# A fixed order for the first transfers, later loads and degree sums held in order, and one-off weight sums moved into the loop, in a two-layer graph kernel

## The chip, the cores and the metric

One Trainium2 chip, one core. The metric is device time of one execution in microseconds (us). Each kernel is run several times and the median is quoted. A kernel is timed in rounds together with the kernel before on the same chip. Ratios and their intervals are taken from the fast runs of both kernels in the same rounds, so they are not quite the ratio of the medians quoted beside them.

In the profile's lines PE is TensorE, DVE VectorE, ACT ScalarE, POOL GpSimd and SP SyncE; a q behind the name marks the issue of a transfer. A line of a timeline gives start and length (us), engine, source line, operation, what is written <- what is read, and the count; brackets give the idle time before it and what ended it. Line numbers are those of the kernel that is profiled. A line of waits gives who waited <- for what: total us, times, longest us.

## The reference, cut to what matters

64 graphs of 256 nodes and 512 features, float32. Two layers, each with a residual and a norm:

```python
# layer 0
deg = jnp.sum(adj, axis=-1, keepdims=True)
agg = jnp.einsum('bij,bjf->bif', adj, x) / jnp.maximum(deg, EPS)
x = _layernorm(x + relu(concat([x, agg]) @ W.T))
# layer 1
q, k = split(x @ Wqk);  v = x @ Wv
agg = jnp.einsum('bij,bjd->bid', adj, k * mask)
w = inv_scale * mask * sum(q * agg)
x = _layernorm(x + softmax(w)[:, :, None] * v)
```

## The kernel before

Matrix products are done with seven block products in place of eight, so each operand needs a few sums and differences of its blocks first. Those of the weights W (and of W1 = [Wqk Wqk^T, Wv]) are made once, on VectorE. Those of x^T and adj are made for each graph on GpSimd. `prepare(g)` also makes the row sums of adj ("degree sums") on ScalarE, which evicts most of TensorE's results as well (it copies them out of the banks in which TensorE accumulates).

The kernel is written in program order, but a scheduler may move an instruction ahead of earlier ones on its engine if it estimates it to be ready sooner. The resulting order on each engine is fixed when the program is built and can be listed before a run ("the built order" below). `tc.keep_in_program_order(i)` keeps i behind what is traced before it on its engine. `tc.issue_after(i)` keeps a block's instructions on i's engine behind i. Both fix an order of issue only, and add no wait.

```python
def load(g):                                            # all in SP's queue
    xTs[g] = ...; nc.sync.dma_start(xTs[g], x_t[g]...)   # 512 KB
    adjs[g] = ...; nc.sync.dma_start(adjs[g], ...)       # 256 KB, bufs=4
    rows[g] = ...; nc.sync.dma_start(rows[g], ...)       # 256 KB, bufs=2
    xs[g] = ...; nc.sync.dma_start(xs[g], ...)           # 512 KB, bufs=3
# ...
for a in range(NA):
    nc.scalar.dma_start(wqk...[a], src)                 # 4 x 512 KB, ACT's queue
load(0)
for h in (0, 1):
    nc.scalar.dma_start(w0[half h], ...)                # 2 x 1 MB, ACT's queue
# ... the mask, 64 KB
nc.sync.dma_start(w1[:, NF:, :], wv...)                 # 1 MB
# 16 matmuls Wqk Wqk^T into 4 banks (each float32 matmul shows as two in the
# profile: 32), evicted into w1 by ScalarE
# ...
def weight_sums(w, name):                               # VectorE, 128x1024 each
    nc.vector.tensor_sub(t1, b12, b11)
    nc.vector.tensor_sub(t2, b22, t1)
    nc.vector.tensor_sub(b12, b22, b12)
    nc.vector.tensor_sub(t4, b21, t2)

def layer0_a(g):
    product(u, A11, B11);  nc.scalar.copy(own[:, 0, :], u)      # first eviction
    product(p5, S1, T1)
    product(u, S2, T2, start=False);  nc.scalar.copy(y[:, 0, :], u)
    product(p2, A12, B21);  nc.vector.tensor_add(own[:, 0, :], p2, own[:, 0, :])
    product(u, S3, T3, start=False);  nc.scalar.copy(y[:, 1, :], u)   # third eviction
    nc.vector.tensor_add(y[:, 1, :], p5, y[:, 1, :])            # first y addition
def layer0_b(g):
    product(u, A22, T4, start=False);  nc.scalar.copy(own[:, 1, :], u)
    product(p5, S4, B22, start=False)
    nc.vector.tensor_add(y[:, 0, :], p5, y[:, 0, :])            # second y addition
# gather_a(g): four tv sums of the values on VectorE, aggregation adj @ values
# norm0(g):    norm, then two masked copies of x1 on ScalarE (layer 1's values)
W0 = weight_sums(w0, "t0_");  prepare(0);  load(1);  W1 = weight_sums(w1, "t1_")
for i in range(B + G + 2):
    load(i + 2)
    layer0_a(i); ...; layer0_b(i); ...; gather_a(i) mixed with layer 1 of graph i - 2
    combine0(i); norm0(i); prepare(i + 1)
```

## Time and profile before

| | before |
|---|---|
| median, us (three runs) | 2011.91 (2011.75 to 2013.03) |
| TensorE busy | 1973.9 of 2010.2 us |
| TensorE idle in the first 80 us | 15 us |
| TensorE idle in the last 50 us | 21 us |
| TensorE idle between | none |

I follow four landmarks in each profile, all start times of TensorE work: the first Wqk matmul, the first matmul of W (graph 0), the first aggregation matmul of graph 0, and that of graph 1. Before, they stand at 6.18, 22.48, 42.74 and 61.20 us. After some 80 us TensorE never waits until the end, so what is won at the landmarks should arrive at the end. The profile's lines are shown and read in the prediction.

### The profile page before, as it was taken

What the parts mean: (1) busy time and instruction counts of PE and PEld (TensorE: products, weight loads), DVE (VectorE), ACT (ScalarE), POOL (GpSimd) and SP (SyncE); (2) the same over time, 40 slices, a digit from 0 to 9 for tenths busy, and PEclk for the clock granted to TensorE, in tenths of its full rate; (3) what the DMA queues carried; (4) which work ended last, traced back from release to release, by engine and by line L of the source; (5) the groups of instructions that cost most, each with busy time, mean ns of one, the idle gap of its engine ahead of it and who ended that gap; (6) DMA issues with size and microseconds to landing.
All of it is one profiled execution on the core that took longest, in us unless ns stands there. A gap on an engine that the chain in (4) does not pass through costs nothing.

```text
span 2010.2 us, 19340 instructions
## 1 busy us (share of the span) xinstructions
PE 1973.9 (98%) x5536; PEld 1030.4 (51%) x5536; DVE 1523.6 (76%) x3184; ACT 673.2 (33%) x1354; POOL 419.0 (21%) x518
## 2 busy tenths in 40 slices
PE   7999999999999999999999999999999999999995
PEld 3555555555555555555555555555555555555552
DVE  3677787777787777787777887777877777877776
ACT  2333333333333332333332333333333333333322
POOL 4121221221221222212212212212212212222100
PEclk9999999999999999999999999999999999999998
DMA  7333333333333333323333333333333333233211
GB/s 241 85 71 94 88 79 94 86 82 91 88 81 92 90 80 84 99 77 86 90 87 86 80 94 89 79 94 85 81 92 90 81 91 86 68 79 79 62 38 53
DMA packets 384872, 174.40 MB, mean 87 GB/s; under 512 B 283776, under 2 KB 349440, under 8 KB 384768
## 3 DMA queue, kind: packets, MB, share of 16 engines
q1 hardware_dynamic: 382624, 168.97, 32.0%
q10 hardware_dynamic: 2144, 4.19, 0.6%
q8 instruction: 46, 0.75, 0.2%
q14 instruction: 58, 0.48, 0.1%
HBM read 105.97 MB, written 33.55 MB: 69 GB/s over the span
## 4 chain that ended last, share of the span: by engine, by line
PE 95%; DVE 1%; ACT 1%; SPq 0%; issue 0%; DMA 0%; DVEq 0%; ACTq 0%
PE mm L142 75%; PE mm L240 19%; SPq L157 0%; PE tp L349 0%; PE tp L335 0%; DVE st L164 0%; DVE o L357 0%; DVE own L272 0%; ACT L341 0%; ACT vals L281 0%; DMA x1T<-sq 0%; ACT rows L177 0%; DVE o L170 0%; DVE own L274 0%; DVE v L325 0%
## 5 line engine op out<-in xcount | busy, mean ns | idle before, releaser
L142 PE MATMUL mm<-w,s 128*128 128x512 f32 x1024 | 481.3, 592 | 0.7 <-ACT v L311 0.7
L142 PE MATMUL mm<-t,s 128*128 128x512 f32 x1024 | 466.2, 597 | 4.8 <-ACT own L197 3.8
L142 PEld LDWEIGHTS mm<-t,s 128*128 128x128 f32 x1024 | 192.3, 190 | 236.7 <-issue 215.5
L142 PEld LDWEIGHTS mm<-w,s 128*128 128x128 f32 x1024 | 194.4, 190 | 192.8 <-issue 163.2
L142 PE MATMUL mm<-w,x1T 128*128 128x512 f32 x512 | 242.5, 596 | 4.1 <-DMA x1T<-sq 4.1
L142 PE MATMUL mm<-w,xT 128*128 128x512 f32 x512 | 242.0, 594 | 0.0
L183 POOL TENSOR_TENSOR sa<-adj 128x128 f32<-128x128 f32 x64 | 47.1, 736 | 781.0 <-PE mm L240 774.3
L134 POOL TENSOR_TENSOR s<-xT 128x256 f32<-128x256 f32 x64 | 47.7, 745 | 703.6 <-PE mm L142 685.8
L240 PE MATMUL mm<-tv,sa 128*128 128x256 f32 x768 | 187.1, 379 | 0.0
L240 PEld LDWEIGHTS mm<-tv,sa 128*128 128x128 f32 x768 | 145.8, 190 | 74.6 <-issue 59.6
L142 PEld LDWEIGHTS mm<-w,xT 128*128 128x128 f32 x512 | 97.9, 191 | 95.8 <-issue 92.4
L272 DVE SCALAR_TENSOR_TENSOR own<-zr,rdeg,own 128x512 f32<-128x512 f32 x128 | 107.6, 841 | 44.4 <-ACT zr L262 44.4
L319 DVE TENSOR_TENSOR v<-mm,v 128x512 f32<-128x512 f32 x64 | 44.3, 692 | 126.3 <-ACT v L318 126.3
L142 PEld LDWEIGHTS mm<-w,x1T 128*128 128x128 f32 x512 | 95.3, 191 | 86.1 <-issue 74.6
L300 DVE SCALAR_TENSOR_TENSOR q<-mm,zr 128x512 f32<-128x512 f32 x128 | 87.7, 685 | 66.1 <-PE mm L142 66.1
L311 ACT COPY v<-mm 128x512 f32<-128x512 f32 x64 | 37.4, 585 | 299.0 <-PE mm L142 299.0
L142 PE MATMUL mm<-t,x1T 128*128 128x512 f32 x256 | 125.5, 612 | 0.7 <-ACT v L318 0.7
L142 PE MATMUL mm<-t,xT 128*128 128x512 f32 x256 | 120.6, 593 | 3.0 <-ACT vals L204 3.0
L240 PE MATMUL mm<-vals,adj 128*128 128x256 f32 x512 | 121.3, 379 | 1.6 <-DVE vals L214 1.6
L357 DVE SCALAR_TENSOR_TENSOR o<-v,probs,x 128x512 f32<-128x512 f32 x128 | 120.3, 959 | 0.1
L240 PEld LDWEIGHTS mm<-vals,adj 128*128 128x128 f32 x512 | 97.1, 190 | 43.2 <-issue 21.5
L214 DVE TENSOR_TENSOR vals<-mm,vals 128x512 f32<-128x512 f32 x64 | 44.3, 692 | 91.8 <-PE mm L142 91.8
(83 smaller groups left out, 2668.6 us busy)
## 6 DMA issues: line engine op xcount, KB each, us to landing
xT<-x_t SPq DMA_DIRECT2D x64, 512.0 KB, 4.1
x<-x SPq DMA_DIRECT2D x64, 512.0 KB, 3.5
x1T<-sq SPq DMA_DIRECT2D x1024, 32.0 KB, 2.0
out<-o SPq DMA_DIRECT2D x64, 512.0 KB, 3.1
adj<-adj_t SPq DMA_DIRECT2D x64, 256.0 KB, 2.6
rows<-adj SPq DMA_DIRECT2D x64, 256.0 KB, 2.6
wqk<-wqk_t ACTq DMA_DIRECT2D x4, 512.0 KB, 8.6
w<-w_t ACTq DMA_DIRECT2D x2, 1024.0 KB, 11.7
```

Source lines behind the costliest of these rows:

```text
L134: eng.tensor_add(s1, a21, a22)
L142: nc.tensor.matmul(ps, a[:, c, :], b[:, c, :], start=start and c == 0, stop=(c == H - 1), skip_group_check=True)
L183: nc.gpsimd.tensor_add(sa[:, 0], a21, a22)
L214: nc.vector.tensor_add(y[:, 0, :], p5, y[:, 0, :])
L240: nc.tensor.matmul(ps[:, k * HF:(k + 1) * HF], sumsA[g - k][a], w[b][:, n, :], start=start and n == 0, stop=True, skip_group_check=True)
L272: nc.vector.scalar_tensor_tensor(own[:, t, :], z[:, t, :], rdeg[:, t:t + 1], own[:, t, :], op0=OP.mult, op1=OP.add)
L300: nc.vector.scalar_tensor_tensor(q, a, 1.0, agg[:, t, :], op0=OP.mult, op1=OP.mult, accum_out=to)
L311: nc.scalar.copy(v[:, 0, :], u)
L319: nc.vector.tensor_add(v[:, 1, :], p5, v[:, 1, :])
L357: nc.vector.scalar_tensor_tensor(o[:, t, :], v[:, t, :], p[:, t, g % G:g % G + 1], x1[:, t, :], op0=OP.mult, op1=OP.add)
```

## The change

Its intent is to have TensorE start earlier and not be held by its first operands. All first transfers go through one queue in the order in which they are used (Wqk, two quarters of W, x^T of graph 0, the other quarters of W, and then the rest). Loads of graph i+2 are issued behind the last of graph i+1, and degree sums of graph i+1 behind graph i's first eviction. The W1 sums move from before the loop to step 1.

```diff
+    def first(out, in_):
+        return tc.keep_in_program_order(nc.sync.dma_start(out, in_))
-    def load(g):
-        xTs[g] = ...  # first of the four
+    def load(g, dma=nc.sync.dma_start):     # adj, rows, x, then x^T through load_t(g, dma)
...
-            nc.scalar.dma_start(wqk...[a], src)
-        load(0)
-        for h in (0, 1):
-            nc.scalar.dma_start(w0[:, h * NF:(h + 1) * NF, :], ...)
+            first(wqk...[a], src)
+        for k in (0, 2):
+            first(w0[:, k * H:(k + 1) * H, :], w0_of[k])
+        load_t(0, first)
+        for k in (3, 1):
+            first(w0[:, k * H:(k + 1) * H, :], w0_of[k])
+        load(0, first)
         mask_sb = ...
-        nc.sync.dma_start(w1[:, NF:, :], wv...)
+        load_t(1, first)
+        load(1, first)
+        loaded = first(w1[:, NF:, :], wv...)
...
-    load(1)
-    W1 = weight_sums(w1, "t1_")
...
         if i + 2 < B:
-            load(i + 2)
+            with tc.issue_after(loaded.ins):
+                loaded = load(i + 2)
+        if i == 1:
+            W1 = weight_sums(w1, "t1_")
...
-            layer0_a(i)
+            began = layer0_a(i)              # returns the first eviction
...
         if i + 1 < B:
-            prepare(i + 1)
+            with tc.issue_after(began.ins):
+                prepare(i + 1)
```

More of the change, by code (lines that the diff above doesn't have):

```diff
@@ L76, in resnorm_kernel, with load_t @@
      open0) = ({} for _ in range(17))
-    def load(g):
-        xTs[g] = pool.tile([P, NF, N], F32, name="xT")
-        nc.sync.dma_start(xTs[g], x_t[g].rearrange("(c p) n -> p c n", p=P))
+    def first(out, in_):
+        return tc.keep_in_program_order(nc.sync.dma_start(out, in_))
+    def load(g, dma=nc.sync.dma_start):
         adjs[g] = pool.tile([P, NT, N], F32, name="adj", bufs=4)
-        nc.sync.dma_start(adjs[g], adj_t[g].rearrange("(t p) i -> p t i", p=P))
+        dma(adjs[g], adj_t[g].rearrange("(t p) i -> p t i", p=P))
         rows[g] = pool.tile([P, NT, N], F32, name="rows")
-        nc.sync.dma_start(rows[g], adj[g].rearrange("(t p) j -> p t j", p=P))
+        dma(rows[g], adj[g].rearrange("(t p) j -> p t j", p=P))
         xs[g] = pool.tile([P, NT, F], F32, name="x", bufs=3)
-        nc.sync.dma_start(xs[g], x[g].rearrange("(t p) f -> p t f", p=P))
+        dma(xs[g], x[g].rearrange("(t p) f -> p t f", p=P))
+        return load_t(g, dma)
+    def load_t(g, dma):
+        if g not in xTs:
+            xTs[g] = pool.tile([P, NF, N], F32, name="xT")
+            return dma(xTs[g], x_t[g].rearrange("(c p) n -> p c n", p=P))
     w0 = const.tile([P, 2 * NF, F], F32, name="w0")
@@ L95, in resnorm_kernel @@
             src = wqk_t.rearrange("(h a p) f -> a p h f", p=P, h=2)[a]
-            nc.scalar.dma_start(wqk.rearrange("p (h a) f -> a p h f", h=2)[a], src)
-        load(0)
-        for h in (0, 1):
-            nc.scalar.dma_start(w0[:, h * NF:(h + 1) * NF, :],
-                                w_t[h * F:(h + 1) * F, :].rearrange("(c p) o -> p c o", p=P))
+            first(wqk.rearrange("p (h a) f -> a p h f", h=2)[a], src)
+        w0_of = w_t.rearrange("(k h p) o -> k p h o", p=P, h=H)
+        for k in (0, 2):
[4 more added lines that the diff above has]
+        load(0, first)
         mask_sb = const.tile([P, NT, B], F32, name="mask_sb")
-        nc.sync.dma_start(mask_sb, mask_t)
-        nc.sync.dma_start(w1[:, NF:, :], wv.rearrange("(c p) o -> p c o", p=P))
+        first(mask_sb, mask_t)
+        load_t(1, first)
+        load(1, first)
+        loaded = first(w1[:, NF:, :], wv.rearrange("(c p) o -> p c o", p=P))
         ident = const.tile([P, P], F32, name="ident")
@@ L196, in layer0_a @@
         product(u, s["A11"], w["B11"])
-        nc.scalar.copy(own[:, 0, :], u)
+        began = nc.scalar.copy(own[:, 0, :], u)
         product(p5, s["S1"], w["T1"])
@@ L206, in layer0_a @@
         open0[g] = u, p5
+        return began
     def layer0_b(g):
```

## The prediction

> **What bounds the kernel now.** I read the page's busy table first, then a table of stretches, then TensorE's waits over the whole run, and last the first 60 us in order of time.
>
> ```profile
> span 2010.2 us, 19340 instructions
> PE 1973.9 (98%) x5536; PEld 1030.4 (51%) x5536; DVE 1523.6 (76%) x3184; ACT 673.2 (33%) x1354; POOL 419.0 (21%) x518
> ```
>
> TensorE is busy for 1973.9 of 2010.2 us. All its idle time together is 36.3 us, or 1.8% of the span: no better order of loads can win more than that without also raising the clock. The table of stretches (columns: stretch, length, busy us and count of each engine, granted TensorE clock, DMA share, GB/s) shows where it lies:
>
> ```profile
> 0.00:10.00 10.00, 3.82 (x5) 1.76 (x6) 0.06 (x1) 0.00 (x0) 2.70 (x11) 1.00 0.79 273
> 20.00:30.00 10.00, 6.31 (x15) 2.29 (x13) 6.60 (x7) 3.92 (x13) 6.43 (x4) 1.00 1.03 349
> 30.00:40.00 10.00, 8.83 (x16) 3.65 (x17) 7.74 (x12) 5.89 (x23) 7.47 (x9) 0.83 0.45 131
> 200.00:1000.00 800.00, 800.00 (x2258) 418.96 (x2257) 619.46 (x1298) 273.45 (x552) 174.40 (x212) 1.00 0.33 86
> 1980.00:2010.20 30.20, 14.24 (x31) 5.85 (x29) 12.35 (x33) 5.47 (x9) 0.00 (x0) 0.73 0.11 42
> ```
>
> The middle is saturated: 800.00 busy in 800.00, at full clock. The idle sits in the first 80 us (about 15 us) and in the last 50 (about 21). The change rewrites the start, so the start is what can be won. TensorE's waits within the first 80 us:
>
> ```profile
> PE mm L113 <- DMA wqk<-wqk_t: 6.2, 1, 6.2
> PE mm L142 <- ACT own L197: 3.8, 1, 3.8
> PE mm L142 <- ACT vals L204: 3.0, 3, 2.1
> PE mm L240 <- DVE vals L214: 1.6, 2, 0.8
> PE mm L142 <- DVE t L122: 0.4, 1, 0.4
> ```
>
> They sum to 15.0 us. In order of time they are the first matmul waiting for Wqk until 6.18; the wait for T1 of W; and the 3.8 us for the eviction of graph 0's first product. ScalarE's timeline tells why that eviction was late:
>
> ```profile
> 26.00 1.06 ACT L116 COPY w<-mm 128x512 f32<-128x512 f32 x2
> 29.02 0.42 ACT L177 ACTIVATE rows<-rows 128x256 f32<-128x256 f32 x1 [1.96 <-DMA rows<-adj]
> 29.34 0.19 ACT L177 ACTIVATION_READ_ACCUMULATOR rows<-rows 128x1 f32 x1
> 29.43 0.40 ACT L177 ACTIVATE rows<-rows 128x256 f32<-128x256 f32 x1
> 29.74 0.19 ACT L177 ACTIVATION_READ_ACCUMULATOR rows<-rows 128x1 f32 x1
> 29.83 0.56 ACT L197 COPY own<-mm 128x512 f32<-128x512 f32 x1
> ```
>
> The product was complete at about 24.4. ScalarE had degree sums of later graphs placed ahead of its eviction, sat idle 1.96 us for their rows to land, and evicted at 29.83. TensorE could not accumulate the next product into that bank before. Eleven loads of rows are issued within the first 60 us, where graphs 0 to 2 would do.
>
> **What the Trainium skill says.** Four places bear on it.
> - "DMA: Bandwidth & Descriptors", section "Queues, rings and completion order": each DMA engine round-robins, packet by packet, between the queue rows that have work, and SP and ACT own one row each. The trace agrees: by 6.0 us the ACT queue had moved 0.54 MB and the SP queue 0.67 MB, so the first 512 KB of Wqk shared the engines with x^T, adj, rows and x, which nothing needs yet.
> - "TensorE: Matmul & The Clock Gate", section "What's actually happening": the array starts at half clock, about 3.4 us of sustained work releases it, an idle window throttles it again, and the window is free-running. The trace agrees: the first six matmuls start 0.85 us apart, later ones 0.43, and after the 3.8 us wait they are 0.85 apart again for some five matmuls, where the clock column shows 0.83 (for the first ten microseconds it shows 1.00, so there I go by the spacing).
> - The same page, "Architectural detail": ScalarE and VectorE are strict FIFO. The eviction behind the late rows, above, is that rule at work.
> - "SBUF — State Buffer", section "SBUF: two separate sides": a VectorE operation with two SBUF inputs and a GpSimd one that reads SBUF exclude each other. Here the same subtraction on W took 1.23 us alone and up to 1.74 beside GpSimd, and GpSimd's 0.72 us sums became 1.7.
>
> **The change part by part.**
>
> (a) Wqk first, in SP's queue alone. In a view of the first 12 us in slices of 0.3 us, the DMA engines moved 0.17 MB up to 3.3 us and then about 385 GB/s. If all of it is Wqk's first quarter (0.52 MB), that is complete at 3.3 + 0.35/0.385 = 4.2, and with its signal the first matmul starts at about 4.4 in place of 6.18. The other quarters follow at 1.4 us each, while a quarter's 8 matmuls take at least 8 x 0.43 = 3.4: no further wait. The 32 matmuls took 22.48 - 6.18 = 16.3 us; with the same warm-up they end at 20.7. Gain 1.8.
>
> (b) W and x^T of graph 0 next. Before, at most eight transfers were outstanding (the mask's issue waited for the first Wqk), so W was issued only at 8.87 and 10.05 and its second half landed at 23.4. Now W's four quarters and x^T are the 2.5 MB behind Wqk's 2.1 MB: the last W quarter lands at about 3.3 + 4.55/0.385 = 15, adj and rows at 16.5, x at 18. VectorE's four subtractions (4 x 1.23, at most 1.74 each) end by 18.5; GpSimd's eight sums (4 x 0.72 + 4 x 0.45 = 4.7, somewhat more with the port shared) by about 19. All lie before 20.7. The wait for T1 goes: from 24.2, when the matmul could have started, to 24.77, it is 0.57.
>
> (c) Degree sums behind the graph's own first eviction. Rows of graphs 1 and up can no longer stand ahead of the eviction of graph 0. It then lies under the S1 x T1 product (4 x 0.43 = 1.72, against 0.56 for a copy), as designed. Without it the next product would have started at 24.77 + 1.72 = 26.49 and not at 30.50: 4.0. And without that idle the clock stays up: the eight matmuls from 30.50 took until 35.70, 5.20 in place of 8 x 0.43 = 3.44: 1.8.
>
> Check of (b) and (c): from 22.48 to graph 0's first aggregation matmul at 42.74 were 20.3 us for 28 matmuls. The floor is 28 x 0.43 = 12.0, plus two exposed evictions that stay (2.56 - 1.72 = 0.84 at vals L204, 2.66 - 1.72 = 0.94 at vals L214), or 13.8. Difference 6.4 = 0.6 + 4.0 + 1.8. So aggregation starts at 20.7 + 13.8 = 34.5, 8.2 us earlier.
>
> (d) Graph 1. Its wait of 2.10 us for vals L204 comes from ScalarE's order: rows (0.6 us), a table load of 1.28, the root, two mask copies, then the eviction. With the rows gone from there the table load can lie under the norm statistics; that may save up to 1.0. I take 0.5. The 0.8 for vals L214 stays.
>
> (e) The T sums of Wqk Wqk^T and Wv move from before the loop to step 1. They are four VectorE operations, about 6 us with the port shared; Wv is last of 8.5 MB and lands at about 25. VectorE is nearly idle between 25 and 34, so most of it fits; one of 1.2 to 1.7 us may stand just ahead of an addition that the aggregation waits for. I take 0.3 of loss.
>
> (f) The middle. Loads keep count and size, and each is needed a step (30 us) after its issue; TensorE has no idle there. Zero. The last 21 us have no loads or degree sums. Zero.
>
> Sum: 1.8 + 6.4 + 0.5 - 0.3 = 8.4, so 2011.9 - 8.4 = 2003.5 us, 0.4% less.
>
> **The rivals.**
> 1. The freed time is absorbed: TensorE starts earlier but then waits for something else, such as the norm of graph 0 or x1^T. For it: graph 1 did wait for ScalarE. Against it: the norm of graph 0 starts from graph 0's aggregation and moves forward with it, and past 80 us TensorE was never idle. It would leave 2 to 4 us of gain: 2008 to 2010.
> 2. One queue in strict order is worse: a load that waits for a buffer (x^T needs its predecessor's products done) blocks the transposes of x1 and the loads behind it at every step. For it: the SP queue already waits 355 us in all for VectorE ahead of x loads. Against it: those waits cost TensorE nothing, with a step of slack. If it did cost 0.3 us a step it would be 60 x 0.3 = 18 us: 2021. Over 2% slower needs 0.7 us at each step.
> 3. Late W1 sums or another static order stall VectorE for 3 to 5 us near step 1: 2007 to 2009.
> 4. More is won: the two short evictions of graph 0 are filled with graph 1's products, or the end closes up. All the start's idle beyond what I count is some 5 us: 1998.
>
> **Range and chances.** The cold clock can cost a microsecond more or less, as its window is free-running; the order of graph 1 gives another one or two either way; a shifted order at the end two or three. So 1999.5 to 2007.5. Faster by 2% would need 40 us, more than all of TensorE's idle: 0.01. Slower by 2% needs the second rival at full strength: 0.02. Within 2%: 0.97.
>
> **What would show it.** Right: the first Wqk matmul near 4.4, the first W matmul near 20.7, no wait for own L197 or T1, clock 1.0 between 20 and 40, the first aggregation matmul near 34.5, and the saturated middle. Wrong: a first matmul still at 6 (one queue doesn't bring the first quarter sooner), any idle of TensorE between 100 and 1900, a wait for W or x^T in graph 0, or waits for the VectorE sums of Wqk and Wv.

## The result, and the profile after

| | before | after |
|---|---|---|
| median, us (four runs each) | 2012.47 | 2004.51 |
| lowest to highest | 2011.75 to 2013.19 | 2003.80 to 2005.38 |
| ratio, 95% interval | | 0.9961 (0.9943 to 0.9978) |
| first Wqk matmul | 6.18 | 4.49 |
| first W matmul | 22.48 | 20.96 |
| first aggregation, graph 0 | 42.74 | 35.23 |
| first aggregation, graph 1 | 61.20 | 54.42 |

The head of the page of the profile after:

```profile
span 2002.7 us, 19342 instructions
PE 1971.7 (98%) x5536; PEld 1030.1 (51%) x5536; DVE 1526.0 (76%) x3184; ACT 677.8 (34%) x1354; POOL 418.0 (21%) x518
```

TensorE's busy time fell by 2.2 us for the same 5536 instructions. Some 1.8 of that are the eight matmuls at half clock that the prediction counted. The rest of the 7.5 us of span is idle time that is gone. TensorE's waits in the first 80 us after the change:

```profile
PE mm L126 <- DMA wqk<-wqk_t: 4.5, 1, 4.5
PE mm L155 <- ACT vals L217: 2.4, 2, 1.7
PE mm L254 <- DVE vals L228: 1.9, 2, 1.2
PE mm L254 <- DVE tv L244: 0.4, 1, 0.4
PE mm L254 <- DVE tv L245: 0.2, 1, 0.2
```

The waits for the first eviction (3.8) and for T1 (0.4) are gone. There are two new ones, for tv sums, and the wait for the second y addition has grown from 1.6 to 1.9 in total. The stretches after (columns as in the prediction) show the clock at 1.00 where the kernel before had 0.83:

```profile
0.00:10.00 10.00, 5.51 (x7) 2.41 (x8) 0.06 (x1) 1.28 (x1) 0.70 (x6) 1.00 0.84 295
20.00:30.00 10.00, 9.70 (x23) 3.99 (x21) 1.50 (x5) 4.23 (x14) 6.80 (x14) 1.00 0.83 289
30.00:40.00 10.00, 7.84 (x21) 3.77 (x22) 8.85 (x11) 1.66 (x4) 3.29 (x4) 1.00 0.35 105
```

Between 20 and 30 us TensorE is now busy 9.70 instead of 6.31. Between 30 and 40 it is busy less than before (7.84 against 8.83): VectorE (8.85) is now in its way, and no half clock stretches the matmuls. VectorE's timeline of that stretch:

```profile
30.96 1.22 DVE L135 TENSOR_TENSOR t<-w 128x1024 f32<-128x1024 f32 x1
32.21 1.23 DVE L136 TENSOR_TENSOR t<-w,t 128x1024 f32<-128x1024 f32 x1
33.36 1.22 DVE L137 TENSOR_TENSOR w<-w 128x1024 f32<-128x1024 f32 x1
34.49 0.68 DVE L228 TENSOR_TENSOR vals<-mm,vals 128x512 f32<-128x512 f32 x1
35.09 1.21 DVE L138 TENSOR_TENSOR t<-w,t 128x1024 f32<-128x1024 f32 x1
36.23 0.41 DVE L244 TENSOR_TENSOR tv<-vals 128x256 f32<-128x256 f32 x1
```

L135 to L138 are the four W1 sums. Three stand ahead of the second y addition (L228), for which the aggregation waits, and the fourth stands between it and the first tv sum (L244), for which the next matmuls wait.

The landmarks add up. From before to after, the stretch up to the first W matmul is 1.52 us shorter; from there to graph 0's aggregation 5.99 shorter (20.26 to 14.27); from there to graph 1's 0.73 longer (18.46 to 19.19); from there to graph 2's (85.19 before, 77.91 after) 0.50 shorter; and the remaining 1925 us 0.22 shorter. The sum is 7.5, the difference of the spans.

### The profile page after: what moved, and what is told of

It reads as the page before. It is cut to its first block, busy times and chain, and to the rows that moved or that the text cites. A ratio compares the mean times of both kernels' runs of the same rounds, so it can differ in the third digit from the quotient of the medians.

```text
span 2002.7 us, 19342 instructions
## 1 busy us (share of the span) xinstructions
PE 1971.7 (98%) x5536; PEld 1030.1 (51%) x5536; DVE 1526.0 (76%) x3184; ACT 677.8 (34%) x1354; POOL 418.0 (21%) x518
## 4 chain that ended last, share of the span: by engine, by line
PE 97%; DVE 1%; SPq 0%; ACT 0%; DMA 0%; issue 0%; DVEq 0%; ACTq 0%
PE mm L155 77%; PE mm L254 19%; PE mm L126 1%; SPq L170 0%; PE tp L363 0%; PE tp L349 0%; DMA wqk<-wqk_t 0%; DVE st L177 0%; DVE o L371 0%; ACT L355 0%; DVE own L286 0%; DVE own L288 0%; DMA x1T<-sq 0%; DVE o L183 0%; ACT vals L295 0%
## 5 line engine op out<-in xcount | busy, mean ns | idle before, releaser
L210 ACT COPY own<-mm 128x512 f32<-128x512 f32 x64 | 37.4, 585 | 227.5 <-PE mm L155 227.5
```

Of the source, the lines that this page charges most:

```text
L210: began = nc.scalar.copy(own[:, 0, :], u)
```

## The experiments

The prediction's time was right, so the question was which part does what. Theory A is the prediction's: each part earns its own share, and holding the degree sums is what removes the 3.8 us wait and the half clock. Rival B: the parts overlap, and the order of the transfers alone already moves the degree sums. A third idea came from the first four runs: late W makes a second bound on VectorE that stands right behind the first one. All kernels gave correct results, five runs each. The kernel before, run beside them, had medians of 2013.15 (the first four kernels), 2012.70 (the next four) and 2012.15 (the last four). The four medians of the kernel before (2012.47 with the changed kernel) differ by 1.0 us, so medians of different groups can't be compared more closely than that. Landmarks are of one profile each, and not always of a typical execution: those of "only degree sums held" (2011.27) and "only first order" (2011.87) are 1.4 and 4.5 us above the median, that of "before, Wqk first" (2004.74) is 1.8 below it:

| kernel | median, us (range) | ratio | Wqk | W | aggr. 0 | aggr. 1 |
|---|---|---|---|---|---|---|
| degree sums free | 2004.17 (2003.88 to 2005.45) | 0.9960 | 5.30 | 21.20 | 35.47 | 54.67 |
| only degree sums held | 2009.85 (2007.38 to 2011.85) | 0.9986 | 6.06 | 21.88 | 41.88 | 60.65 |
| only first order | 2007.42 (2005.82 to 2011.87) | 0.9973 | 4.67 | 21.26 | 36.67 | 60.99 |
| graph 0 beside Wqk | 2002.72 (2002.62 to 2003.16) | 0.9951 | 5.03 | 20.57 | 34.48 | 52.30 |
| W1 sums early | 2005.70 (2003.14 to 2006.98) | 0.9966 | 4.72 | 20.12 | 35.52 | 54.31 |
| later loads free | 2002.69 (2002.65 to 2005.58) | 0.9955 | 4.81 | 20.26 | 34.53 | 53.29 |
| W1 sums in gaps | 2002.59 (2001.56 to 2004.41) | 0.9952 | 4.76 | 21.47 | 35.38 | 53.20 |
| gaps, masked copies later | 2001.98 (2001.60 to 2002.96) | 0.9949 | 4.54 | 21.10 | 35.00 | 52.34 |
| before, Wqk first | 2006.51 (2004.74 to 2008.25) | 0.9971 | 6.20 | 21.66 | 35.57 | 55.09 |
| block put back | 2008.81 (2006.83 to 2012.35) | 0.9985 | 4.32 | 20.86 | 41.67 | 59.50 |
| as graph 0 beside Wqk, queues exchanged | 2003.82 (2003.69 to 2003.87) | 0.9958 | 6.15 | 22.85 | 36.75 | 54.58 |
| before, sums held, W1 in gaps | 2004.32 (2004.24 to 2005.93) | 0.9962 | 6.19 | 21.92 | 37.24 | 55.07 |

### Degree sums free

```diff
-            with tc.issue_after(began.ins):
-                prepare(i + 1)
+            prepare(i + 1)
```

> The changed kernel with the degree sums of later graphs free to go anywhere on ScalarE. Theory A (the prediction's: holding them is what removes the 3.8 us wait for graph 0's first eviction): the wait comes back, the clock drops again, first aggregation matmul near 41, about 6 us lost, 2010 us. Rival B (the two parts overlap: once the transfers come in order, the scheduler itself places the sums behind the eviction; in the built order of this kernel they do stand behind it): first aggregation matmul near 35, 2004.5 us within 0.7.

2004.17 us, and the same 14.27 us from W to graph 0's aggregation as in the changed kernel. Theory A falls in this point: with the transfers in order and the later loads held, holding the degree sums adds nothing that these runs can see.

### Only degree sums held

The kernel before, with only this:

```diff
-            layer0_a(i)
+            began = layer0_a(i)
...
-            prepare(i + 1)
+            with tc.issue_after(began.ins):
+                prepare(i + 1)
```

> The kernel before with nothing but the degree sums held behind the graph's own first eviction. Theory A and rival B both: first Wqk matmul stays near 6.2 and the 0.4 us wait for T1 stays, the 3.8 us wait and the half clock after it go, first aggregation matmul near 42.7 - 5.8 = 36.9, 2012.5 - 5.8 = 2006.7 us. If the order of the transfers were needed for it too (rival C: the eviction is then held by something else that lands late): 2010 to 2012.

The wait for the first eviction did vanish, but little was won: 2009.85 us, with graph 0's aggregation at 41.88 in the profiled run. Theory A and rival B did not have this. Rival C had nearly the time, but by an eviction held up by something else, and the eviction was not held up. A new wait took the place of the old one:

```profile
PE mm L142 <- DVE vals L205: 2.6, 1, 2.6
```

VectorE's timeline of this kernel shows why (L122 to L125 are weight sums, at 30.05 and later those of W1; L205 is the first y addition):

```profile
30.05 1.40 DVE L122 TENSOR_TENSOR t<-w 128x1024 f32<-128x1024 f32 x1
...
34.16 1.47 DVE L125 TENSOR_TENSOR t<-w,t 128x1024 f32<-128x1024 f32 x1
...
36.09 0.67 DVE L202 TENSOR_TENSOR own<-mm,own 128x512 f32<-128x512 f32 x1
36.68 0.68 DVE L205 TENSOR_TENSOR vals<-mm,vals 128x512 f32<-128x512 f32 x1
```

VectorE started the eight sums of W and W1 only when W's second half had landed, at 23.43, and was through at 35.6. The first y addition was ready to go when its eviction was done at 32.87, and came at 36.68. The S4 x B22 product writes on into the bank that this addition reads, so TensorE waited, and then ran that product at half clock (3.59 us for four matmuls instead of 1.88). In the kernel before, the same eight sums end at 35.95. This second bound lay there too, hidden behind the first.

### Only first order

The changed kernel without either hold, and with the W1 sums before the loop:

```diff
-            with tc.issue_after(loaded.ins):
-                loaded = load(i + 2)
+            loaded = load(i + 2)
...
-            with tc.issue_after(began.ins):
-                prepare(i + 1)
+            prepare(i + 1)
...
     prepare(0)
+    W1 = weight_sums(w1, "t1_")
```

> The changed kernel with only the first transfers in one queue in their order; later loads and degree sums free, W1 sums before the loop as before. Theory A: only the start and T1 are won, 1.7 + 0.6, 2010 us. Rival B: nearly everything is won, first matmul at 4.5, first aggregation matmul near 35.5 (W1 sums stand before the addition for it), 2004.5 to 2006.5; the sums of graphs far ahead may cost graph 1 up to 1 us on ScalarE.

2007.42 us, between the two expectations and with a wide spread (6.1 us). Graph 0's aggregation comes at 36.67: the eviction is not blocked, so the order of transfers alone removes that block. What is lost is lost in graph 1, 24.3 us from aggregation to aggregation instead of 19.19. Eleven loads of rows are issued in the first 60 us again (four in the changed kernel), and their degree sums stand among graph 1's evictions: 12 pairs of instructions between 38 and 53 us, and a wait of 2.6 us for graph 1's third eviction. But this is the profile of the slowest of the five runs, and most of what it loses is clock: TensorE is busy 1976.5 us against 1971.7 in the changed kernel, 4.8 of the 7.1 us by which the span is longer, as the half clock follows two of its waits. The other four runs (2005.82 to 2008.31) lost less.

### Graph 0 beside Wqk, and the queues exchanged

```diff
+        load_t(0, nc.scalar.dma_start)
+        load(0, nc.scalar.dma_start)
         w0_of = ...
-        load_t(0, first)
...
-        load(0, first)
```

> The changed kernel with the four loads of graph 0 issued from ScalarE's queue at the start, beside Wqk in SP's. If sharing the DMA engines set the first matmul's time before: it comes near 6.2 again (from 4.5), and the end is 1.5 to 1.7 us later, 2006.1. If the first transfer's own latency set it (rival): 4.5 stays and 2004.5.

The first matmul came at 5.03, inside the range of kernels that don't share (below), and the kernel was 1.8 us faster than the changed one, not slower. Its built order differs in one more thing than I had meant: the scheduler now puts the W1 sums earlier in VectorE's order, the last one done 1.9 us ahead of the second y addition. It shows neither 1.15 us nor a tv wait: 13.91 us from W to aggregation, and 17.82 from graph 0's to graph 1's.

The exchange put Wqk in ScalarE's queue and graph 0's loads in SP's:

```diff
-            first(wqk...[a], src)
+            nc.scalar.dma_start(wqk...[a], src)
...
+        load_t(0, first)
+        load(0, first)
```

> As the kernel with graph 0's loads beside Wqk at the start, but with the queues exchanged: Wqk from ScalarE's queue, graph 0's loads from SP's, as the kernel before had them; all else as in the changed kernel. If which queue carries Wqk matters beside the sharing: first matmul near 6.1 as in the kernel before. If sharing alone gives 5.0 (what the other way round showed) and 6.1 was chance: 5.0. The end hardly moves with it, 2003 to 2004.5, as the start of the clock's warm-up differs between runs more than this.

6.15 here, as the first branch of the expectation has it. Taken over all profiles: in the eight kernels whose Wqk has the transfer engines to itself at the start, the first matmul starts at 4.32 to 5.30 (mean 4.70); in the six with another stream beside it (these two, the kernel before, and the three experiments made from it), at 6.06 to 6.20 in five and at 5.03 in one. So kernels that share start about 1.3 us later on average. That one of six escaped it, I can't explain. The end does not show it here: this kernel reached W latest of all, at 22.85, and finished in 2003.82. Its W1 sums, too, were placed early by the scheduler (the last done at 32.39, the second y addition at 36.01), so from W to graph 1's aggregation it takes 31.73 us against 33.46 in the changed kernel, which makes up for most of the 1.9 us by which it is later at W.

### W1 sums early

```diff
     prepare(0)
+    W1 = weight_sums(w1, "t1_")
...
-        if i == 1:
-            W1 = weight_sums(w1, "t1_")
```

> The changed kernel with the W1 sums traced before the loop again; loads and degree sums stay held. In the built order all four W1 sums now stand ahead of the addition that graph 0's aggregation waits for, where the changed kernel has three of them. Theory (VectorE's W1 sums are the new wait): first aggregation matmul 1.1 us later than in the changed kernel, near 36.4, the two short waits for the tv sums (0.6) gone, so 0.5 us slower or the same, 2004.5 to 2005.5. Rival (the move is what protects graph 0): 2007 to 2009, as in the kernel with only the order of transfers.

2005.70 us, just above the upper end of the theory's range and short of the rival's. From W to aggregation it takes 15.40 us, 1.1 more than in the changed kernel, as expected of the fourth sum ahead of the addition. The waits for tv sums did not go as expected: one of 0.72 us is left. From graph 0's to graph 1's aggregation it takes 18.79, 0.4 less.

This kernel and the one with only the first order have the same wait of 2.3 us for the second y addition, and the clock answered differently. Aggregation of graph 0, and the stretch from 30 to 40 us, here and then with only the first order:

```profile
35.52 1.13 PE L254 MATMUL mm<-vals,adj 128*128 128x256 f32 x4 [2.28 <-DVE vals L228]
36.49 0.59 PE L254 MATMUL mm<-tv,sa 128*128 128x256 f32 x2
```

```profile
36.67 1.25 PE L254 MATMUL mm<-vals,adj 128*128 128x256 f32 x4 [2.29 <-DVE vals L228]
37.75 1.19 PE L254 MATMUL mm<-tv,sa 128*128 128x256 f32 x2
```

0.59 against 1.19 us for the same two matmuls. A wait of this length may or may not bring the half clock. That fits the spread of the runs: the four experiments whose profile shows a wait of 2.3 us or more after the first matmul spread by 3.8 to 6 us, and the two with the narrowest spreads (0.2 and 0.5 us) have none above 1.5. It isn't a proof: two kernels without such a wait ("before, Wqk first" and "W1 sums in gaps", longest waits 1.96 and 1.47) spread by 3.5 and 2.9.

### Later loads free

```diff
-            with tc.issue_after(loaded.ins):
-                loaded = load(i + 2)
+            loaded = load(i + 2)
```

> The changed kernel with the later loads not held behind one another; degree sums held, first transfers in order. The built order of the start is the same but for one load of rows. Theory (either hold is enough, since only degree sums far ahead do harm): as the changed kernel, 2004.5 within 0.7. Rival (holding the loads is what keeps the engines clear): 2006 to 2008.

2002.69 us, no slower than the changed kernel and 1.1 below the theory's range. The rival falls. From W to aggregation it takes 14.27 us as there; 0.7 us of its lead is a luckier start (W at 20.26). With "degree sums free": either hold is enough, and both together are not better than one. That graph 1 suffers without either is seen in one profile ("only first order") and not clear in the times: with the W1 sums in the same place, 2007.42 without holds and 2005.70 with both, and the ranges overlap.

### W1 sums in gaps, and masked copies later

The W1 sums are made two at a time where VectorE is idle in graph 1:

```diff
-        if i == 1:
-            W1 = weight_sums(w1, "t1_")
 # in layer0_a(1), behind the first y addition:
+        with tc.issue_after(added.ins):
+            nc.vector.tensor_sub(t1, b12, b11);  nc.vector.tensor_sub(t2, b22, t1)
 # in gather_a(1), behind its last tv sum:
+        with tc.issue_after(t4_done.ins):
+            nc.vector.tensor_sub(b12, b22, b12);  nc.vector.tensor_sub(t4, b21, t2)
```

> The changed kernel with the four W1 sums put in two idle stretches of VectorE in graph 1 (behind the y addition of graph 1's first part, and behind the last tv sum of graph 1). If the W1 sums cost the changed kernel the waits 1.15 instead of 0.79 at the y addition, and 0.43 + 0.20 at the tv sums: first aggregation matmul 0.4 us earlier, near 34.8, those two waits gone, and 1.0 to 1.8 us off the end: 2003.0. Rival (they only delay what is waited for anyway, the norm of graph 0): 2004.5.

TensorE's waits of its first 80 us:

```profile
PE mm L126 <- DMA wqk<-wqk_t: 4.8, 1, 4.8
PE mm L171 <- ACT vals L233: 2.1, 2, 1.5
PE mm L272 <- DVE vals L246: 1.6, 2, 0.8
```

The tv waits are gone and the addition costs 0.8 twice, the exposed floor of the prediction. From the first W matmul to graph 1's aggregation it takes 31.73 us against 33.46 in the changed kernel. So where the changed kernel has its W1 sums costs 1.7 us. The two kernels with exchanged or shared queues take the same 31.73. The median shows 1.9, but the ranges overlap (2001.56 to 2004.41, 2003.80 to 2005.38). (The expected 34.8 for the aggregation was missed because this run reached W late, at 21.47; from W on it is 13.91.)

The next one adds, for graph 0 only, that the two masked copies stand behind graph 1's third eviction:

```diff
 # norm0(0) leaves the masked copies out; in layer0_a(1):
-        nc.scalar.copy(y[:, 1, :], u)
+        third = nc.scalar.copy(y[:, 1, :], u)
+        with tc.issue_after(third.ins):
+            masked(0)
```

> As the kernel with the W1 sums in gaps, and the two masked copies of graph 0's x1 stand behind graph 1's third eviction on ScalarE, not ahead of it. If the table load, root and masked copies ahead of that eviction are the 1.5 to 1.7 us wait of graph 1: it falls to 0.7, another 0.8 to 1.0 off: 2002.0. Rival (the root's wait for the norm statistics alone holds it): no further gain, 2003.0.

```profile
PE mm L275 <- DVE vals L249: 1.7, 2, 0.9
PE mm L171 <- ACT vals L233: 1.4, 2, 0.7
```

The wait for the third eviction of graph 1 falls from 1.5 to 0.7 as expected, and the stretch from graph 0's to graph 1's aggregation from 17.82 to 17.34, so some of it is given back. At the end 2001.98 us, 0.6 less, which the two ranges do not separate. It does beat the changed kernel: its slowest run (2002.96) is faster than that one's fastest (2003.80).

### The kernel before, with Wqk first

```diff
-            nc.scalar.dma_start(wqk...[a], src)
+            tc.keep_in_program_order(nc.sync.dma_start(wqk...[a], src))
...
-        load(0)
+        with tc.issue_after(last_wqk):
+            load(0)
```

> The kernel before with Wqk's four loads ahead of graph 0's loads in SP's queue, and nothing else; W still comes as two halves in the other queue. Additive theory (the prediction's first term stands by itself): first matmul 4.5 to 5.3, W's first matmul near 21, and 1.3 to 1.8 off the end, 2011.0. Rival (VectorE's eight sums of W and W1, which start when W's second half lands near 23.4, are the second bound behind the eviction): first matmul early, but first aggregation matmul still 41 to 42.7, and nothing won at the end, 2012 to 2012.7.

2006.51 us; both expectations were wrong, since I had overlooked what else moved. With Wqk out of ScalarE's queue, W is first there and is issued at once:

```profile
0.73 1.05 ACTq L102 DMA_DIRECT2D w<-w_t  x2
```

So Wqk shares the transfer engines with W, and the first matmul stays at 6.20. But VectorE has W's second half at 14.37 instead of 23.40, the four sums of W end at 20.2, and the W1 sums at 27.9. The built order also has graph 0's first eviction ahead of graph 1's degree sums. From W to aggregation it takes 13.91 us, the floor. An earlier W, together with the order that the scheduler then chose, was thus worth about 6 us with the first matmul unmoved.

### Block put back

The changed kernel, with the degree sums of graphs 1 and 2 ahead of graph 0's first eviction on purpose:

```diff
-        began = nc.scalar.copy(own[:, 0, :], u)
+        # g == 0: behind degrees(1) and degrees(2)
+        with tc.issue_after(early["last"].ins):
+            began = nc.scalar.copy(own[:, 0, :], u)
```

> The changed kernel with the degree sums of graphs 1 and 2 put on purpose ahead of graph 0's first eviction on ScalarE, as the kernel before had them; transfers as in the changed kernel. If that order is what cost 3.8 us of waiting and the clock after it: the rows of graph 2 land near 26.5, eviction near 27.5, a wait of about 3.5 us for it and half clock after it, first aggregation matmul 39 to 41, 2008.5 to 2010.5. Rival (the block was never the bound): 2004.5.

ScalarE, then TensorE:

```profile
27.80 0.42 ACT L192 ACTIVATE rows<-rows 128x256 f32<-128x256 f32 x1 [4.55 <-DMA rows<-adj]
...
28.62 0.56 ACT L219 COPY own<-mm 128x512 f32<-128x512 f32 x1
```

```profile
29.28 2.77 PE L155 MATMUL mm<-t,s 128*128 128x512 f32 x4 [3.11 <-POOL sa L205]
```

ScalarE idles 4.55 us for rows of graph 2, evicts at 28.62 (about 27.5 was expected), and TensorE goes on at 29.28, at half clock (the column shows 0.66 between 30 and 40 us). The view names GpSimd as the releaser; the eviction ended at 29.18, 0.1 us ahead, which is the release that fits. From W to aggregation it takes 20.81 us, 6.5 more than in the changed kernel and close to the 20.26 of the kernel before. The end is 4.3 us later: with graph 0 late, the W1 sums no longer stand in anyone's way, and graph 1's stretch is 17.83 instead of 19.19.

### The kernel before, sums held and W1 sums in gaps

The edits of "only degree sums held" and of "W1 sums in gaps" together, transfers untouched.

> The kernel before with the degree sums held behind the eviction, and the W1 sums in the gaps of graph 1; all transfers as before. If the W1 sums ahead of the y addition were what kept the kernel with only the hold from winning (its 2.6 us wait and the half clock after it): W's first matmul to first aggregation falls from 20.0 to about 15.3, first aggregation matmul near 37.3, 2006.5. Rival (late W itself is the bound): first aggregation 40 or later, 2010.

```profile
37.24 1.13 PE L259 MATMUL mm<-vals,adj 128*128 128x256 f32 x4 [0.79 <-DVE vals L233]
```

Expected at 37.3, and from W to aggregation 15.32 where 15.3 was expected. At 2004.32 us (2006.5 was expected) it is as fast as the changed kernel, without a single transfer moved. This settles the second bound: take away the block on ScalarE and the W1 sums on VectorE, and the old order of the transfers costs only the late start and a wait of 1.2 us for T1. "W1 sums in gaps", which has the new order and the holds on loads as well, took 2002.59: with both blocks gone, these are worth some 1.7 us, not clear of noise (2001.56 to 2004.41 against 2004.24 to 2005.93).

## Why the prediction was right, and where a step was not

The prediction said 2003.5 in 1999.5 to 2007.5, and "same" within 2%; 2004.51 was measured. Step by step:

- **(a) Wqk first, gain 1.8.** The first matmul was placed within 0.1 us. What arrives at W is less: the eight kernels with Wqk alone reach W at 20.12 to 21.47 (mean 20.90), the six with sharing at 20.57 to 22.85 (mean 21.89), so 1.0 on average and 1.52 in the pair of profiles. The term was too large because the half-clock phase doesn't simply move with the first matmul: it lasted for four to seven matmuls in kernels with identical first transfers, and the earliest first matmul (4.32) gave W at 20.86, where one at 4.72 gave 20.12.
- **(b) W early, gain 0.6.** The direct wait for T1 was that. The step was undersized in what it missed: late W, with the W1 sums behind it, held VectorE until 35.95 in the kernel before, a second bound right behind the ScalarE block. "Only degree sums held" ran into it, and the kernel with Wqk first won some 6 us from W's earlier landing and the built order that came with it. (One reading behind the term was loose: the W sum of 1.23 us "alone" had a GpSimd sum issued 0.09 us behind its start, which then took 1.72. The first W sum after the change, at 11.71 with GpSimd idle, took 1.23 too.)
- **(c) The eviction, 4.0 + 1.8.** The size is right: from W to aggregation 5.99 us were won against 6.4 for (b) and (c) together, and 6.35 in the kernels with the W1 sums out of the way. The block put back costs 6.5. The cause was ascribed wrongly: the prediction gave all of it to the hold on the degree sums. That hold is not needed (free: 2004.17) and not enough (alone: 2009.85). With W early, the scheduler puts the sums of later graphs behind the eviction by itself, even where the loads of their rows are free ("only first order" and "before, Wqk first").
- **(d) Graph 1, gain 0.5.** Its wait fell from 2.10 to 1.73, 0.4 (to 1.47 with the W1 sums out of the way). ScalarE's table load now starts right behind the second eviction, at 45.41, and is over before the norm statistics are there (46.85), as predicted. Right.
- **(e) W1 sums moved, loss 0.3.** This is the mis-sized term: 1.7. The prediction expected them to fit between 25 and 34 us; the built order placed the first behind the first y addition, at 30.96, though Wv had landed near 26.0 (issued at 16.61, 9.4 us to landing). One of the four, it said, might stand ahead of an addition; in fact three stand ahead of it and the fourth behind it, ahead of the tv sums.
- **(f) The middle and the end, zero.** 0.22 us over 1925. Right, though from graph 2's aggregation to the end single profiles differ by 2.2 us (1923.8 to 1926.1).

That the sum came within 1.0 us of the time is in part luck. Term (e) was 1.4 short, and 0.50 in graph 2 and the 0.22, which stand in no term, gave half of that back.

The rivals named there: the second (the queue in strict order costs each step) did not occur, as TensorE is busy 800.00 of 800.00 us from 200 on after the change too. The third (W1 sums stall VectorE) occurred at about half the strength given. The first and the fourth did not happen as described, though the last five microseconds that the fourth spoke of are partly there to be had, as the kernel at 2001.98 shows.

Two things stay open: why one of six shared starts was quick, and which of the two effects of early W, the sums or the order that the scheduler then chose, was worth how much in the kernel with Wqk first; no run separates them.

## What to carry to other kernels

When one wait is due to go, look for the chain that would hold the same engine next, here eight sums on VectorE that began when W landed. Taking away the first alone won 3.3 us of some 8. Where a scheduler orders the engines, a change of transfers is also a change of every engine's order: list the order of each engine for each variant before you ascribe a gain to a line of the diff. And one-off sums that fit into an engine's idle time on paper belong where nothing waits behind them; here that was worth 1.7 us of a prologue of 80.

## What the Trainium skill lacked or had wrong

- "TensorE: Matmul & The Clock Gate", section "What's actually happening", gives about 3.4 us for the idle window after which the clock is halved. Here the half clock followed a wait of 2.29 us in one profile (two matmuls in 1.19 us, not 0.59) and did not follow one of 2.28 us in another. In the first it set in at 37.55 us, 0.9 us after the wait had ended, and lasted 6.8 us; in the kernel before, at 31.65 us, 1.15 us after the wait of 3.77 had ended, and lasted 3.4 us. Waits of 2.10 us and less brought no half clock in the first 80 us of any profile. The page says that the window is free-running; it doesn't say that a wait shorter than the window may or may not halve the clock. That the run times spread with it (3.8 to 6 us in the four experiments with a wait of 2.3 us or more) is not proven.
- The clock column of a profile can show 1.00 while matmuls start 0.85 us apart, as in the first ten microseconds of the kernel before. The same page, in "Seeing it yourself", says only in general that the clock events of a trace can't be fully trusted, not that the column can miss the slow start.
